# Block products for the output projection, and scores joined with the neighbouring group's attends, in a four-layer graph network on one core

## The chip, the cores and the metric

The kernel runs on one core of a Trainium2 chip. The core has five engines that run side by side and wait for one another through semaphores: TensorE (PE) for matrix products into PSUM (eight banks of 128 x 512 fp32), VectorE (DVE), ScalarE (ACT), GpSimd (POOL), and SyncE (SP), which here issues nearly all DMAs. The metric is device time of the one core in microseconds (us), the median of several executions. The profile is of one further execution.

## The reference

The input `x` holds 128 batches of 128 nodes with 512 features; `adj` is a 128 x 128 weighted adjacency matrix. Four layers follow one another, each with a residual sum and a layer norm, all in fp32:

```
# layer 0: graph convolution
x = layernorm(x + (adj @ x) @ W0 + bias0)
# layer 1: graph attention
h = x @ W1;  e = leaky_relu(h@a1 + (h@a2)^T) * adj
x = layernorm(x + elu(softmax(e) @ h + beta * h))
# layer 2: max over features; adj stands for both weights
A = adj @ x;  C = adj @ x + b
x = layernorm(x + max_j relu(A_j + (C - A)))
# layer 3: attention with 8 heads of 64, masked where adj == 0
q, k, v = split(x @ w_qkv)
o = softmax(mask(q k^T / 8)) @ v
o = o @ w_proj + b_proj
x = layernorm(x + o + layernorm(o) * gamma + beta)
```

## The kernel before

**Work.** A batch is one tile of 128 x 512. The work of a batch up to the end of layer 2 is `batch` (L906): load, `mixed_rows` or `mixed` (`adj @ x`, L276 to L309), a product with W0 (`product`, L269: four matmuls of 512 columns accumulated in one bank), layer norm (`layernorm_sums`, L243), two row sums with the attention vectors (L942), then layer 1 with a product of W1, layer 2 with one matmul (L974), and a transpose of the result (L989) that goes out to DRAM for layer 3. The tile itself is then written out to DRAM (`spill`, L892), apart from that of the last 8 batches (`KEPT`), which frees its buffer; `fetch` (L899) brings it back at the end.

**Layer 3** works on groups of four batches (31 of them, and two of two at the end). `gather` collects the four transposed tiles as a 2 x 2 block matrix, and forms four differences of blocks on GpSimd (L680). `section` (L685) computes q, k and v, each as seven products of blocks instead of eight (the Strassen-Winograd scheme: seven products of half-size blocks, sums of weights prepared once by `weight_sums`, copies on ScalarE at L743, sums on VectorE at L757, and a last copy at L813). `tiled` (L824) and `score` compute the scores of the four batches: two heads at a time in the two 64-row halves of the TensorE array. Each batch then adds the mask (L1006), takes the softmax (L1013 to L1034), and turns the result through DRAM (L1037 to L1046, `to_rows` and `from_rows`). `attend` (L862) multiplies with v, two batches in one block, in two 64-column halves of the array. `usual` (L1074) copies the output, multiplies by `w_proj` (`product`, four matmuls of 512 columns for each batch), adds the bias on VectorE (L1079), and ends with the two layer norms and the store; `last` (L1101) is the same for the last batch, cut in halves.

**Order.** The order of every engine is fixed when the kernel is built, by a planner (`Plan`, L63). Each chain of steps is a generator. `yield use(engine, work, buffer)` asks for an engine for so many estimated microseconds, and for a free buffer of a kind in `BUFS`. The planner always grants the request that can start first; among those that can start together the urgent one, then the lowest rank (usually the batch number). For TensorE it counts a request as ready up to 1 us (`MARGIN`) later than estimated. On the chip each engine runs its list in that order and waits for what isn't ready.

**Buffers.** Ten tiles `x` hold batches between load and spill; `t` (5) are scratch tiles; `qk` (4) and `v` (4) hold two groups; `z`, `e`, `et`, `eT` serve the attention of layer 1, `pt` the turned softmax. `layernorm_sums` writes its squares, which nobody reads, into a `t` tile (L248), and L942 does so too.

## Time and profile before

| | us |
|---|---|
| median of 3 runs (3197.40 to 3198.48) | 3198.22 |
| the profiled execution, its own time | 3195.69 |
| span of that execution | 3193.9 |
| mean granted TensorE clock, share of full speed | 0.992 |
| DMA: share of the 16 engines' time in the queue of SP | 46.7% |
| TensorE: three products of 512 columns a batch (L273), busy | 1376 |
| TensorE: blocks of q, k and v (L706), busy | 1257 |
| GpSimd: additions and subtractions of tiles (L266, L680), busy | 702 |
| VectorE: L942, 256 instructions, mean of one | 0.881 |

A line of the profile's groups names the source line, the engine, the operation, the tile that it writes and those that it reads (without their numbers), the shape, and the count of instructions; then the busy time of all, the mean of one in nanoseconds, and the idle time of the engine just ahead of them with what ended it. An fp32 matmul is recorded as two instructions, and as two weight loads ("PEld"). "128\*128" is the whole array, "64\*128" a half by rows, "128\*64" a half by columns. Matmuls are pipelined: the busy time of one overlaps that of the next, so the distance from start to start in the timeline is the better measure of cost.

### The profile page before, as it was taken

To read this page: it belongs to the slowest core of one execution; us is meant where nothing else is said; L and a number is where in the kernel's file an instruction comes from. 1 tells how busy PE (TensorE), PEld (TensorE's weight loads), DVE (VectorE), ACT (ScalarE), POOL (GpSimd) and SP (SyncE) were. 2 spreads that over 40 slices of the span, in tenths; PEclk is the share of its full clock that TensorE was granted. 3 is DMA by queue.
4 is the path that set the end of the run, shared out by engine and by line. 5 is a ranking of instruction groups with operands and counts; after the bars stand their busy time and mean duration, and the time that the engine had idled before them with its cause. 6 is when DMAs were issued, how large, how long until landed. Compare 5 with 4: busy or idle time off the path is not lost. (4 is left out here: it accounts for less than half of the span.)

```text
span 3193.9 us, 46192 instructions
## 1 busy us (share of the span) xinstructions
PE 3118.6 (98%) x14295; PEld 2063.0 (65%) x14295; DVE 2504.9 (78%) x5281; ACT 1768.6 (55%) x5143; POOL 1114.2 (35%) x1178
## 2 busy tenths in 40 slices
PE   8999999999999999999999999999999999999997
PEld 4566666666666676666666666666666666657785
DVE  7777878878878877787778787778678887877776
ACT  4565556555556655465645565546465556555553
POOL 5523343223343233333233423252323442342222
PEclk9999999999999999999999999999999999999998
DMA  4535455434563453555354644454534564344342
GB/s 164 146 111 153 116 152 150 134 122 136 141 167 116 135 153 100 165 145 144 121 132 123 170 123 141 121 146 128 160 103 133 139 175 123 117 126 115 101 138 94
DMA packets 766757, 429.47 MB, mean 134 GB/s; under 512 B 570032, under 2 KB 652336, under 8 KB 766512
## 3 DMA queue, kind: packets, MB, share of 16 engines
q1 hardware_dynamic: 766368, 426.26, 46.7%
q8 instruction: 115, 1.88, 0.3%
q14 instruction: 130, 1.06, 0.1%
q10 hardware_dynamic: 144, 0.26, 0.0%
HBM read 221.84 MB, written 204.54 MB: 133 GB/s over the span
## 5 line engine op out<-in xcount | busy, mean ns | idle before, releaser
L216 POOL TENSOR_TENSOR rstd<-ve,neghalf 128x1 f32<-128x1 f32 x640 | 402.2, 633 | 1473.2 <-ACT ve L255 1176.5
L273 PE MATMUL ps<-w_sb,yT 128*128 128x512 f32 x1952 | 874.9, 595 | 9.3 <-ACT yT L292 7.2
L273 PEld LDWEIGHTS ps<-w_sb,yT 128*128 128x128 f32 x1952 | 369.3, 191 | 410.6 <-issue 386.6
L706 PE MATMUL ps<-xT,wqkv_sb 128*128 128x256 f32 (+1 forms) x2112 | 474.0, 373 | 0.8 <-POOL xT L680 0.8
L273 PE MATMUL ps<-wproj_sb,v 128*128 128x512 f32 x1016 | 458.7, 603 | 14.6 <-ACT v L1061 9.9
L706 PEld LDWEIGHTS ps<-xT,wqkv_sb 128*128 128x128 f32 x2112 | 390.1, 190 | 79.0 <-issue 26.5
L1027 ACT ACTIVATE qk<-qk,nmx 128x128 f32<-128x128 f32 x1008 | 391.5, 391 | 25.8 <-DVE nmx L1013 25.5
L743 ACT COPY t<-ps 128x512 f32<-128x512 f32 (+1 forms) x297 | 168.5, 568 | 414.0 <-PE ps L706 230.7
L706 PE MATMUL ps<-xT,wsum_sb 128*128 128x256 f32 (+1 forms) x1584 | 357.4, 376 | 11.0 <-ACT t L743 10.9
L273 PEld LDWEIGHTS ps<-wproj_sb,v 128*128 128x128 f32 x1016 | 195.2, 193 | 251.1 <-issue 228.3
L706 PEld LDWEIGHTS ps<-xT,wsum_sb 128*128 128x128 f32 x1584 | 295.2, 192 | 76.5 <-issue 22.4
L942 DVE SCALAR_TENSOR_TENSOR t<-x,wa_rows 128x512 f32<-128x512 f32 x256 | 225.4, 881 | 56.6 <-ACT x L260 33.8
L250 ACT ACTIVATE t<-x,nm 128x512 f32<-128x512 f32 x263 | 187.8, 714 | 137.9 <-DVE nm L247 129.6
L680 POOL TENSOR_TENSOR xT<-xT 128x512 f32<-128x512 f32 (+1 forms) x132 | 173.1, 1315 | 220.2 <-PE ps L706 138.4
L706 PE MATMUL ps<-wqkv_sb,xT 128*128 128x256 f32 x1024 | 242.9, 380 | 0.0
L757 DVE TENSOR_TENSOR qk<-ps,t 128x256 f32<-128x256 f32 (+2 forms) x297 | 175.3, 620 | 84.5 <-PE ps L706 37.9
L706 PEld LDWEIGHTS ps<-wqkv_sb,xT 128*128 128x128 f32 x1024 | 192.2, 190 | 54.5 <-issue 25.2
L266 POOL TENSOR_TENSOR x<-x,beta_sb 128x512 f32<-128x512 f32 x128 | 178.8, 1399 | 115.9 <-DVE t L989 93.2
L260 ACT ACTIVATE x<-x,nmr,rstd 128x512 f32<-128x512 f32 x263 | 214.0, 814 | 8.8
L266 POOL TENSOR_TENSOR x<-x,bias_sb 128x512 f32<-128x512 f32 x128 | 176.1, 1386 | 118.0 <-PE ps L300 107.1
L266 POOL TENSOR_TENSOR xr<-xr,v 128x512 f32<-128x512 f32 x120 | 163.6, 1364 | 111.0 <-DVE v L1079 32.5
L1037 DVE STREAM_TRANSPOSE pt<-qk 128x1024 f32<-128x1024 f32 x128 | 158.4, 1238 | 42.0 <-DMA p_d<-pt 41.5
(109 smaller groups left out, 4833.0 us busy)
## 6 DMA issues: line engine op xcount, KB each, us to landing
p_d<-pt SPq DMA_DIRECT2D x128, 512.0 KB
qk<-p_d SPq DMA_DIRECT2D x128, 512.0 KB
x_d<-t SPq DMA_DIRECT2D x244, 256.0 KB
xT<-x_d SPq DMA_DIRECT2D x512, 64.0 KB
x<-in_x SPq DMA_DIRECT2D x127, 256.0 KB
x_s<-x SPq DMA_DIRECT2D x120, 256.0 KB
xr<-x_s SPq DMA_DIRECT2D x120, 256.0 KB
out<-xr SPq DMA_DIRECT2D x120, 256.0 KB
```

The costliest lines, as they stand in the source:

```text
L216: nc.gpsimd.tensor_tensor(rstd, ve, neghalf, op=ALU.pow)
L250: nc.scalar.activation(buf(b_sq, D), xb, AF.Square, bias=nm, accum_out=squares)
L260: nc.scalar.activation(xb, xb, AF.Identity, bias=nmr, scale=rstd)
L266: nc.gpsimd.tensor_tensor(dst, dst, other, op=ALU.add)
L273: nc.tensor.matmul(p, lhs(k), rhs(k), start=(k == 0), stop=(k == K - 1))
L680: nc.gpsimd.tensor_tensor(gr.xT[:, out, :, :n], gr.xT[:, a, :, :n], gr.xT[:, b, :, :n], op=ALU.subtract)
L706: nc.tensor.matmul(to, lhs, rhs, start=first and j == 0 and k == 0, stop=final and k == 1, skip_group_check=True,)
L743: nc.scalar.copy(held[1], p)
L757: nc.vector.tensor_tensor(c, a, b, op=ALU.add)
L942: nc.vector.scalar_tensor_tensor(buf(b_s, D), xb, 1.0, wa_rows[:, j, :], op0=ALU.mult, op1=ALU.mult, accum_out=gr.s[:, b, j : j + 1],)
L1027: nc.scalar.activation(pr[:, j, :], pr[:, j, :], AF.Exp, bias=nmx[:, j : j + 1], accum_out=sums[:, j : j + 1],)
L1037: nc.vector.transpose(pt.rearrange("p c h s -> p h c s"), pr.rearrange("p h (c r) -> p h c r", c=Q))
```

## The change

**The projection in pairs.** Two neighbouring batches of a group form the 2 x 2 block matrix that `section` forms of four. The scheme of seven products is taken out of `section` as `seven`, the block differences out of `gather` as `differences`, and `pair_product` uses both for a pair: seven products of 128 x 256 by 256 x 256. The last four batches (`PLAIN`) keep the four wide matmuls. The bias is now added on GpSimd. One block of `w_proj` is replaced by a difference when its sums are made, and loaded again ahead of the last two pairs (`wproj_again`).

**One tiled block.** `tiled` for group g now also runs the attends of group g-1 behind the scores of g, having waited for the softmax rows of all of g-1. In the last five groups (`APART`) the attends stay apart, each batch on its own.

**Buffers and ranks.** `x` goes from 10 to 7, `yT` from 4 to 3, `t` from 5 to 7; `z`, `e`, `et`, `eT` share 8 tiles `u`; the turned softmax takes two `t` tiles and goes out in two DMAs. At the start six batches are loaded into three idle `v` buffers (`GUESTS`). Squares overwrite the bank or tile read just before; L942's output goes into one fixed tile. The softmax takes a rank later by 10 (`SOFT`); only the last 4 batches stay unspilled. The small results of a norm share one tile. Estimates of some steps are changed, and TensorE's margin is 0.7 us from 2900 us on.

The core of the diff:

```diff
+APART = 5
-KEPT = 8
+KEPT = 4
+SEVEN1 = 0
+SEVENP = 1
+PLAIN = 4
+GUESTS = 6
+CLOSE = 2900
+SOFT = 10
+PROJ = 0
...
-    "x": 10, "xr": 2, "yT": 4, "z": 1, "e": 1, "et": 1, "eT": 3, "t": 5, "xT": 2, "v": 4,
-    "qk": 4, "pt": 1,
+    "x": 7, "xr": 2, "yT": 3, "u": 8, "t": 7, "xT": 2, "v": 4,
+    "qk": 4, "y": 0, "c": 2,
...
-        early = min(MARGIN, r["ready"] / 20) if engine == "PE" and order else 0.0
+        spare = MARGIN if r["ready"] < CLOSE else 0.7
+        early = min(spare, r["ready"] / 20) if engine == "PE" and order else 0.0
...
-        b_sq = yield use("ACT", 1.2, "t")
-        squares = small.tile([P, 1], F32, name="squares")
-        nc.scalar.activation(
-            buf(b_sq, D), xb, AF.Square, bias=nm, accum_out=squares
-        )
-        give(b_sq)
...
+        yield use("ACT", 1.2)
+        nc.scalar.activation(buf_or_bank(unread), xb, AF.Square, bias=nm, accum_out=squares)
+        give(unread)
...
-        for i in range(8, BUFS["x"]):
+        for i in range(8, BUFS["x"] + GUESTS):
             yield from load(i)
...
-            plan.start(tiled(gr, None, range(size)), rank)
-            for b in range(0, size, ATTENDS):
-                bs = tuple(range(b, min(b + ATTENDS, size)))
-                for bs in (bs,) if g < len(sizes) - 1 else tuple((b,) for b in bs):
-                    plan.start(attend(gr, bs), first)
+            plan.start(tiled(gr, groups.get(g - 1) if g - 1 < len(sizes) - APART else None, range(size)), rank)
+            if g >= len(sizes) - APART:
+                for b in range(size):
+                    plan.start(attend(gr, (b,)), first)
...
+    def seven(rank, bx, wide, time, multiply, into, finished, have, pieces, slow=0.0):
...
+        x = bank(bx, D)[:, :wide]
+        multiply(x, A11, B11, True)
+        m1 = keep(x)
+
+        bz = yield use("PE", time, "ps", late=0.2)
+        z = bank(bz, D)[:, :wide]
+        multiply(z, A12, B21, True, True)
+        plan.start(release(add(z, m1, 0, 0), bz), rank)
+
+        yield m1[0]
+        yield have[T2]
+        yield use("PE", time, late=0.2)
+        multiply(x, S2, T2)
+        u2 = keep(x)
...
+    def differences(blocks, have, used, time, rank):
+
         for out, a, b, when, t in (
             (T3, B22, B12, None, T3), (T1, B12, B11, None, T1),
...
+            yield use("POOL", time, urgent=True)
+            nc.gpsimd.tensor_tensor(blocks(out), blocks(a), blocks(b), op=ALU.subtract)
+            done(have[t], 0.1)
+
+    def pair_product(rank, s, ready, blocks, release, out, finished):
...
+        def multiply(p, w, block, first=False, final=False):
+            w, t = weight(s, w), blocks(block)
+            for k in range(2):
+                nc.tensor.matmul(
+                    p, t[:, k], w[:, k, :], start=first and k == 0, stop=final and k == 1,
+                    skip_group_check=True,
+                )
...
+        plan.start(differences(blocks, have, used, 0.75, rank), rank)
+        token = yield use("PE", 0.0, "c", late=0.0)
+        bx, *slots = yield use("PE", 0.87, lambda: ("ps", "t", "t"), late=0.2)
+        out.extend(buf(slot, D) for slot in slots)
+        out.append(slots)
+        yield from seven(
+            rank, bx, D // 2, 0.87, multiply, into, finished, have, lambda *tiles: [tiles],
+        )
+        give(token)
...
+        yield i + SOFT
         yield use("DVE", 1.22)
...
-        yield use("SP", 0.5, late=4.0)
-        to_rows(pt.rearrange("p c h s -> p c (h s)"), scratch)
-        give(bt)
+        for j, pt in enumerate(turned):
+            yield use("SP", 0.5, late=4.0 * j)
+            to_rows(
+                pt.rearrange("p c h s -> p c (h s)"),
+                scratch[:, :, j * H // 2 * S : (j + 1) * H // 2 * S],
+            )
+        for bt in halves:
+            give(bt)
...
+        if SEVENP and gr.first + 2 * h < NB - PLAIN:
+            if h not in gr.extra:
+                gr.extra[h] = None
+                plan.start(projection(gr, h, i + PROJ), i + PROJ)
+            done(gr.copied[h])
+            yield gr.projected[h][b % 2]
+            o, slot = gr.p[h][b % 2], gr.p[h][2][b % 2]
+            biased = Event()
+            plan.start(pool_add(o, bproj_sb, biased), i)
+            yield biased
+            yield from normed(i, o, lambda: give(slot), fetched)
+        else:
+            yield from (last if i == NB - 1 else usual)(
+                i, oT, v, lambda: gr.read(("v", b // 2), 2), fetched
+            )
```

## The prediction

> **What bounds the kernel now.** I read busy times first, then the groups by shape, the granted clock and waits, then TensorE's timeline.

> ```profile
> PE 3118.6 (98%) x14295; PEld 2063.0 (65%) x14295; DVE 2504.9 (78%) x5281; ACT 1768.6 (55%) x5143; POOL 1114.2 (35%) x1178
> PE   8999999999999999999999999999999999999997
> ```

> TensorE is busy in every slice, so a microsecond of its work is a microsecond of time, unless a new wait replaces it. Its idle time is 75.3 us (3193.9 - 3118.6). The waits that release it sum to 14 us before 110 us, 41 us up to 3100 and some 11 us behind, and none stands out: the longest total is 10.9 us ("ACT t L743").

> Part of the start, from the table by stretches (length, then busy time and count of PE, PEld, DVE, ACT and POOL, then clock, DMA share, GB/s): 5.5 us idle, and a clock of 0.89.

> ```profile
> 60.00:100.00 40.00, 34.52 (x112) 18.66 (x112) 34.88 (x89) 23.34 (x58) 16.17 (x16) 0.89 0.19 60
> ```

> Busy time of pipelined matmuls overstates, so I price TensorE from one start to the next in its timeline (start, length, line, count of instructions; one fp32 matmul shows as two):

> ```profile
> 1546.89 3.60 PE L273 MATMUL ps<-w_sb,yT 128*128 128x512 f32 x8
> 1550.42 3.84 PE L856 MATMUL ps<-qk 64*128 64x128 f32 x64
> 1554.19 1.12 PE L974 MATMUL ps<-x,adjT 128*128 128x512 f32 x2
> 1555.15 3.60 PE L273 MATMUL ps<-w_sb,yT 128*128 128x512 f32 x8
> 1558.59 1.95 PE L281 MATMUL ps<-eT,x 128*128 128x128 f32 x16
> 1560.37 1.89 PE L706 MATMUL ps<-wqkv_sb,xT 128*128 128x256 f32 x8
> 1562.10 7.03 PE L273 MATMUL ps<-w_sb,yT 128*128 128x512 f32 x16
> ...
> 1581.01 3.62 PE L706 MATMUL ps<-xT,wqkv_sb 128*128 128x256 f32 x16
> 1584.56 1.97 PE L877 MATMUL ps<-qk,v 128*64 128x128 f32 x32
> 1586.46 1.99 PE L706 MATMUL ps<-xT,wqkv_sb 128*128 128x256 f32 x8
> 1588.29 3.60 PE L273 MATMUL ps<-wproj_sb,v 128*128 128x512 f32 x8
> ```

> A 512-column product is 3.44 us (1555.15 to 1558.59). Ahead of a tiled block it is 3.53 (1546.89 to 1550.42).

> **Part 1, the projection.** Two batches now cost two L273 products, 6.88 us. The seven products are two matmuls of 256 columns each, four recorded instructions: the form that the value section has in groups of two.

> ```profile
> 3088.99 1.03 PE L706 MATMUL ps<-wqkv_sb,xT 128*128 128x256 f32 x4
> 3089.86 1.95 PE L706 MATMUL ps<-xT,wqkv_sb 128*128 128x128 f32 x16
> ```

> That is 0.87 us each, 6.09 for seven, so a pair saves 0.79. All but the last four batches go this way: 62 x 0.79 = **48.7 us** off TensorE.

> [...] A pair goes from 16 weight loads to 28, all on full rows, and the row of L706 prices one at 190 ns[...]. The row decides: eight instructions of 256 columns last 1.73 us (1560.37 to 1562.10), eight of 512 columns 3.44, with as many loads. Per column the one costs what the other does, so the doubled loads are hidden; I take 48.7.

> The other engines, from the groups by shape:

> ```profile
> L1079 DVE TENSOR_TENSOR v<-ps,bproj_sb 128x512 f32<-128x512 f32 x127 | 86.8, 684 | 51.2 <-PE ps L273 48.7 <-ACT x L260 1.7
> L757 DVE TENSOR_TENSOR v<-ps,t 128x256 f32<-128x256 f32 x6 | 2.5, 410 | 1.1 <-ACT t L743 0.7 <-PE ps L706 0.4
> L743 ACT COPY t<-ps 128x256 f32<-128x256 f32 x18 | 6.6, 369 | 14.5 <-PE ps L706 7.6 <-DVE nm L247 5.9 <-DVE qk L757 0.8
> L680 POOL TENSOR_TENSOR xT<-xT 128x256 f32<-128x256 f32 x8 | 6.2, 771 | 17.9 <-DMA xT<-x_d 10.0 <-PE ps L706 7.8
> ```

> VectorE loses 124 bias adds (-84.8 us) and gets three sums a pair, 186 x 0.41 = +76.3. ScalarE gets four copies a pair, 248 x 0.37 = +91, to 1860 (59%). GpSimd gets the bias adds (124 x 1.386 = 172), four differences a pair (248 x 0.771 = 191) and four weight sums (6): 1114 to 1483, 47%. None reaches TensorE's time. The seven products wait on one another's copies; sections of other groups and layers 0 to 2 lie between, as they do for L706 now.

> GpSimd's additions slow VectorE. Sorting the timeline by whether a large GpSimd add overlaps it, L942 takes 1.23 us beside one (87 of 256) and 0.70 without, L1091 1.42 against 0.75, L1087 1.08 against 0.74. Large GpSimd work grows by half (about 700 to 1060 us), so half as many again are hit: 43 x 0.53 + 25 x 0.67 + 28 x 0.34, about 50 us with L1034. [...] VectorE's sum is about 2567 (82% of the forecast) by the row[...]. Either stays under TensorE, so I charge nothing; without that cover the 50 us would be paid.

> **Part 2, scores and attends in one block.** Sixteen full-size 128-column matmuls take 1.78 us (1558.59 to 1560.37), so 0.89 us per batch of scores or attends. A score block of four takes 3.77, 0.21 over; the product ahead pays 0.09 and the matmul behind 0.10 (1554.19 to 1555.15 is 0.96; 0.86 elsewhere). Together 0.41. An attend block of two takes 1.90, 0.12 over, and its neighbours pay 0.10 each: 0.32. One place has them adjoining:

> ```profile
> 3068.63 1.16 PE L856 MATMUL ps<-qk 64*128 64x128 f32 x16
> 3069.72 3.71 PE L877 MATMUL ps<-qk,v 128*64 128x128 f32 x64
> 3073.37 14.00 PE L273 MATMUL ps<-wproj_sb,v 128*128 128x512 f32 x32
> ```

> Scores 1.09 (0.20 over), attends 3.65 (0.09 over), 0.10 on either side: 0.49. A group now pays 0.41 + 2 x 0.32 = 1.05, so merging saves 0.56. There are 28 merges, 15.7 us. In the last five groups attends go singly, seven more blocks, 2.2 back. Net **13.5 us**. Now 11 score blocks are broken after three batches for want of banks. Unbroken blocks would return 4 us more; were each merged block broken into single attends, 28 x 1.2 = 34 would be lost. VectorE empties two banks in 1.37 us (681 ns each, L1006) while TensorE uses two per 0.89 us of scores, then one per 0.89 of attends, so the banks nearly keep up: I leave the share broken as it is.

> The block has a new wait: group g's attends stand behind the softmax rows of all four batches and group g+1's q and k. They come a group period (100 us) later, holding q/k and v buffers longer. Behind the wait on TensorE is everything in its order; the planner fills it with layers 0 to 2 of seven batches.

> **Part 3, buffers.** Pairing each line's k-th execution (batches 24 to 111), a batch needs 109 us from load to L934 and 132 from L934 to its spill (L895). Most of the 109 is waiting after landing: the work itself, load 3.9, L300 0.86, L303 0.70, two DMA hops of 4.1 and 3.9, product 3.44, sum 0.7, is some 18. So a buffer is needed for about 150 us. Ten give 250, seven 171 at the new pace: 21 us of slack, enough, cost 0.

> Until 100 us TensorE idles 14 us, mostly in waits for the first attention matrices (L281) with no other batch loaded. Six guests in the v buffers make 13 loads instead of 10: three more first-layer products, 3 x (0.89 + 3.44) = 13 us of filling. Ends 0 and 13; they load behind much else, so I take **6**.

> **Small edits.** The softmax's output goes out in two DMAs: 128 more issues on SP at 0.38 us, with SP often waiting itself (L336), and two transposes of about 0.70 for one of 1.24, +20 us of covered VectorE. Only the last group shows it: +1 us (0 to 3). Squares written over read banks hold a bank some 1.5 us longer and relieve t; no row shows ScalarE writing there. The nearest, its reads (581 ns against 714 into SBUF), put it between -0.13 and +0.13 us each: 0 where ScalarE has 40% spare. Softmax at a later rank and four more spilled batches: 0.

> **Sum.** 48.7 + 13.5 + 6 - 1 = 67 us off the profiled execution's 3195.7 (span 3193.9, 1.8 around it): 3128.5. The median shown is 2.5 above that execution, so **3131**.

> **Rivals.** *B, half goes into waits.* Whole-group waits, banks held longer and the products' mutual waits double the 41 us of mid-run idle: 3131 + 41 = 3172. For it: fewer batches in flight.[...]
> *C, slower: x starves.* A buffer is held longer than seven batch periods of the old pace, 7 x 24.97 = 174.8 us. From there holding time / 7 is the pace; at 178 us it gives 25.4 x 128 = 3255. For it: 132 us of the chain were seen with ten buffers and a busier GpSimd lengthens them. Against: the wait of L942 to L961 (66 us on average, 38 at least) has slack.
> *D, more.* The start fills wholly (7 more) and the mid-run idle halves (20): 3104. For it: gaps now come from single late copies and DMAs. Against: nothing in the change shortens these chains.

> **Chances.** Forecast 0.55, B 0.22, C 0.08, D 0.15. A measurement here tells 0.2% (6.4 us) from nothing; B's far end touches it. So faster 0.90, same 0.02, slower 0.08. The range reaches from a little under D to a little over B: 3100 to 3176. It takes in the broken blocks (+34) and leaves out C.

> **What would show it.** Right: TensorE still at 97% or more; seven times four instructions per pair at 0.87; some 28 scores-to-attends changes without full-size work between; 50 us more VectorE. Wrong: loads waiting on spills with TensorE idle on L300 (C), TensorE waiting for copies of the projection or for the softmax's DMA inside the merged block (B), 256-column products above 0.95[...], or merged blocks in pieces.

## The result, and the profile after

The changed kernel takes 3157.86 us (median of four, 3154.84 to 3159.49) beside 3198.14 for the kernel before on the same chip: a ratio of 0.9873, interval 0.9856 to 0.9890. It is 40 us faster. The forecast was 67 us faster, 3131, with a range of 3100 to 3176; the time lies inside, and the gain is 60% of the one forecast. The profiled execution shows the same difference: its span is 3153.0 us instead of 3193.9, 40.9 less.

The page of the changed kernel, busy times and TensorE by slices:

```profile
span 3153.0 us, 48736 instructions
PE 3058.7 (97%) x15039; PEld 2205.0 (70%) x15039; DVE 2550.1 (81%) x5470; ACT 1851.3 (59%) x5391; POOL 1512.5 (48%) x1554
PE   9899999999999999999999999999999999999996
```

TensorE's busy time fell by 59.9 us. Its idle time (span less busy) rose by 19.0, from 75.3 to 94.3. At an equal granted clock (0.992) these two make up the 40.9.

The idle time by place, from the table by stretches of the changed kernel (length, busy time and count of PE, PEld, DVE, ACT and POOL, then clock, DMA share, GB/s):

```profile
0.00:200.00 200.00, 181.85 (x627) 104.67 (x628) 154.30 (x371) 100.71 (x237) 104.73 (x103) 0.97 0.49 145
200.00:3053.00 2853.00, 2802.01 (x13901) 2042.08 (x13900) 2316.51 (x4947) 1697.50 (x4982) 1364.24 (x1407) 1.00 0.50 137
3053.00:3153.00 100.00, 74.80 (x514) 58.27 (x513) 79.30 (x154) 53.13 (x173) 43.52 (x46) 0.90 0.42 129
```

That is 18.2 us idle in the first 200, 51.0 between, 25.2 in the last 100. The kernel before, cut the same way, has 15.2, 39.1 and 21.0:

```profile
200.00:3093.90 2893.90, 2854.82 (x13079) 1890.90 (x13078) 2284.43 (x4791) 1625.44 (x4762) 997.06 (x1056) 1.00 0.48 135
3093.90:3193.90 100.00, 78.99 (x501) 57.31 (x500) 70.73 (x138) 40.86 (x120) 29.25 (x35) 0.89 0.36 116
```

So 3 us of the added idle time is in the first 200, 12 in the middle and 4 at the end.

TensorE's waits in the changed kernel (line that waited, releaser; total, times, longest in us):

```profile
PE ps L304 <- DMA x<-in_x: 14.6, 9, 2.8
PE ps L869 <- ACT t L732: 11.0, 7, 3.2
PE ps L277 <- DMA yT<-x_d: 7.3, 5, 2.9
PE ps L277 <- DMA wproj_sb<-in_L_gnn_w_proj: 6.0, 1, 6.0
PE ps L277 <- ACT yT L296: 5.1, 2, 3.3
PE ps L1102 <- ACT x L264: 4.8, 6, 1.8
PE ps L825 <- ACT u L732: 4.4, 4, 3.1
```

The first is new. With ten buffers no first-layer matmul (L304, which was L300) waited for its load; with seven, nine did. Pairing executions as before, a batch now needs 45 us from its load to its first sum (L1027, which was L934; 109 before): most of the lead is used up, and some loads come just too late. The third was 0.5 us before. The fourth is new too, the reload of the weight block near the end. The products of the projection (L825) wait 4.4 us in the whole run.

### The profile page after: what moved, and what is told of

The parts are those of the page before. It is cut to its first block, busy times and chain, and to the rows that moved or that the text cites. A ratio compares the mean times of both kernels' runs of the same rounds, so it can differ in the third digit from the quotient of the medians.

```text
span 3153.0 us, 48736 instructions
## 1 busy us (share of the span) xinstructions
PE 3058.7 (97%) x15039; PEld 2205.0 (70%) x15039; DVE 2550.1 (81%) x5470; ACT 1851.3 (59%) x5391; POOL 1512.5 (48%) x1554
## 3 DMA queue, kind: packets, MB, share of 16 engines
q8 instruction: 120, 1.97, 0.3%
## 5 line engine op out<-in xcount | busy, mean ns | idle before, releaser
L228 POOL TENSOR_TENSOR sums<-sums,neghalf 128x1 f32<-128x1 f32 x383 | 256.9, 671 | 590.7 <-ACT sums L260 566.9
L869 PE MATMUL ps<-xT,wqkv_sb 128*128 128x256 f32 (+1 forms) x2112 | 478.8, 375 | 2.6 <-DVE t L307 2.2
L869 PEld LDWEIGHTS ps<-xT,wqkv_sb 128*128 128x128 f32 x2112 | 393.5, 191 | 88.6 <-issue 32.9
L869 PE MATMUL ps<-xT,wsum_sb 128*128 128x256 f32 (+1 forms) x1584 | 356.9, 376 | 12.9 <-ACT t L732 8.5
L869 PEld LDWEIGHTS ps<-xT,wsum_sb 128*128 128x128 f32 x1584 | 294.9, 192 | 77.3 <-issue 20.5
L732 ACT COPY t<-ps 128x512 f32<-128x512 f32 x279 | 160.7, 578 | 257.9 <-PE ps L869 168.2
L228 POOL TENSOR_TENSOR n<-n,neghalf 128x1 f32<-128x1 f32 x257 | 173.2, 674 | 215.6 <-DVE n L223 194.5
L258 ACT ACTIVATE ps<-x,sums 128x512 f32<-128x512 f32 x244 | 167.0, 684 | 133.7 <-DVE sums L256 133.0
L869 PE MATMUL ps<-wqkv_sb,xT 128*128 128x256 f32 x1024 | 241.5, 380 | 0.0
L1034 DVE SCALAR_TENSOR_TENSOR unread_dve<-x,wa_rows 128x512 f32<-128x512 f32 x244 | 212.1, 869 | 24.6 <-ACT x L264 19.6
L746 DVE TENSOR_TENSOR qk<-ps,t 128x256 f32<-128x256 f32 (+1 forms) x279 | 168.5, 635 | 76.7 <-PE ps L869 41.6
L869 PEld LDWEIGHTS ps<-wqkv_sb,xT 128*128 128x128 f32 x1024 | 193.5, 190 | 44.5 <-issue 17.7
L270 POOL TENSOR_TENSOR t<-t,bproj_sb 128x512 f32<-128x512 f32 x124 | 174.9, 1415 | 102.3 <-ACT t L792 68.2
L264 ACT ACTIVATE x<-x,sums 128x512 f32<-128x512 f32 x247 | 201.0, 814 | 8.3
L270 POOL TENSOR_TENSOR xr<-xr,t 128x512 f32<-128x512 f32 x124 | 175.5, 1417 | 40.3 <-DMA xr<-x_s 31.2
L1156 ACT ACTIVATION_READ_ACCUMULATOR qk<-qk,nmx 128x1 f32 x1008 | 191.0, 189 | 0.0
```

The costliest lines, as they stand in the source:

```text
L228: nc.gpsimd.tensor_tensor(rstd, ve, neghalf, op=ALU.pow)
L258: nc.scalar.activation(buf_or_bank(unread), xb, AF.Square, bias=nm, accum_out=squares)
L264: nc.scalar.activation(xb, xb, AF.Identity, bias=nmr, scale=rstd)
L270: nc.gpsimd.tensor_tensor(dst, dst, other, op=ALU.add)
L732: nc.scalar.copy(held[1], p)
L746: nc.vector.tensor_tensor(c, a, b, op=ALU.add)
```

## The experiments

The draws of chip differ (the kernel before has medians of 3192 to 3198 beside these runs), so kernels are compared by their ratio to the kernel before. All twelve are in one table, each with its profiled execution. "Idle" is TensorE's in the first 200 us, between, and in the last 100. "Half clock" is worked out from the trace's record of TensorE's clock, which holds two values, 1.0 and 0.5 of full speed: it is half of the busy time that falls into stretches at 0.5, as an estimate of the time lost in them (a product of L825 in the changed kernel takes 1.86 us to the next start at 0.5, 3111.73 to 3113.59, and 0.87 at 1.0). "Work" is the busy time without that loss.

| kernel | ratio (interval) | span, us | PE busy | half clock | work | idle |
|---|---|---|---|---|---|---|
| before | 1 | 3193.9 | 3118.6 | 19.0 | 3099.6 | 15 + 39 + 21 |
| changed | 0.9873 (0.9856 to 0.9890) | 3153.0 | 3058.7 | 18.1 | 3040.6 | 18 + 51 + 25 |
| e1, wide projection | 1.0059 (1.0042 to 1.0076) | 3212.5 | 3112.1 | 27.5 | 3084.6 | 15 + 62 + 24 |
| e2, attends apart | 1.0151 (1.0131 to 1.0170) | 3237.7 | 3104.7 | 33.9 | 3070.8 | 19 + 85 + 30 |
| e3, third part alone | 1.0149 (1.0120 to 1.0178) | 3237.3 | 3133.5 | 29.2 | 3104.3 | 14 + 65 + 25 |
| e4, softmax not late | 1.0031 (1.0023 to 1.0039) | 3196.4 | 3072.0 | 31.3 | 3040.7 | 16 + 82 + 26 |
| e5, before, 7 x | 1.0064 (1.0049 to 1.0079) | 3212.6 | 3117.8 | 20.1 | 3097.7 | 33 + 33 + 28 |
| e6, before, 9 x | 1.0173 (1.0157 to 1.0188) | 3245.8 | 3126.4 | 28.1 | 3098.3 | 25 + 68 + 27 |
| e7, before, softmax late | 1.0226 (1.0211 to 1.0242) | 3268.4 | 3142.4 | 42.8 | 3099.6 | 14 + 90 + 21 |
| e8, before, joined block | 1.0071 (1.0054 to 1.0088) | 3215.6 | 3113.3 | 28.7 | 3084.6 | 15 + 53 + 34 |
| e9, before, margin 0.99 | 1.0012 (1.0005 to 1.0018) | 3195.1 | 3119.1 | 22.4 | 3096.7 | 15 + 40 + 20 |
| e10, changed, margin 0.99 | 0.9890 (0.9875 to 0.9905) | 3160.0 | 3060.9 | 21.5 | 3039.4 | 18 + 52 + 29 |
| e11, changed, margin 1.01 | 0.9954 (0.9939 to 0.9969) | 3176.0 | 3057.8 | 17.4 | 3040.4 | 26 + 60 + 33 |
| e12, changed, reload early | 0.9868 (0.9853 to 0.9883) | 3155.4 | 3067.5 | 27.5 | 3040.0 | 19 + 48 + 21 |

Kernels with the same matmuls have the same work within 3 us: 3096.7 to 3099.6 for the kernel before and e5, e6, e7 and e9, and 3039.4 to 3040.7 for the changed one and e4, e10, e11 and e12 (which differs by one pair).

### Each part undone (e1 to e4)

**e1.** The projection alone goes back:

```diff
-SEVENP = 1
+SEVENP = 0
```

> The changed kernel with its projection back in four wide matmuls for each batch, the bias on VectorE and no reload of a weight block. Theory T (the part prices on TensorE hold, and the 27 us short of the forecast were lost at the start, in loads of x and at the end): TensorE's busy time rises by 48 to 3107, and the median by 48 less the 6 us of the reload's wait, to about 3200. Theory R (the seven products give part of their gain back through waits on one another's copies and through GpSimd's added work): without them idle time falls too, by 15 or more, and the median is 3185 or less.

Busy time rose by 53.4 us, idle time by 6. The ratio went up by 0.0186, 59 us of 3198. R, which had the seven products give some of their gain back in waits, falls: idle time rose without them, although the wait for the reload is gone. Of the 53 us of busy time 9 are half clock. TensorE's work rose by 44.0, which is 5 less than the 48.7 of the forecast; the rest of the 59 us is waiting and what the clock loses by it, and can be the draw of the order (below).

**e2.** All attends apart, one block for each batch:

```diff
-APART = 5
+APART = 40
```

> The changed kernel with every batch's attends in a block of their own, in all groups. By the prices of the tile shapes on TensorE a merged group costs 0.49 us and one in five blocks 0.41 + 4 x 0.32 = 1.69, so 28 x 1.2 = 34 us more: T expects 3192, with TensorE's busy time up by about 30. R (the merged block pays for its price with idle time, since it waits for four softmax rows): idle time falls by 10 or more and the median stays under 3182. If moving the attends also shifts what waits for what, the idle time rises instead and the median goes over 3205.

The ratio rose by 0.0278, 89 us. T had 34, R is wrong in sign, and the last sentence of the expectation is what came: idle time rose, by 39 us. Busy time rose by 46, of which 30 are work, as T priced it, and 16 are half clock. One wait of e2 is more than the added idle time:

```profile
PE ps L970 <- DMA qk<-p_d: 54.3, 28, 4.8
```

In the changed kernel the attends waited for that DMA twice, 2.4 us in all, and both times in the last groups, where they stand apart. No joined block waited for it: behind the scores of the next group, the attends find the softmax landed.

**e3.** Both large parts undone; what is left is the third part.

```diff
-SEVENP = 1
+SEVENP = 0
...
-            plan.start(tiled(gr, groups.get(g - 1) if g - 1 < len(sizes) - APART else None, range(size)), rank)
-            if g >= len(sizes) - APART:
-                for b in range(size):
-                    plan.start(attend(gr, (b,)), first)
+            plan.start(tiled(gr, None, range(size)), rank)
+            for b in range(0, size, ATTENDS):
+                bs = tuple(range(b, min(b + ATTENDS, size)))
+                for bs in (bs,) if g < len(sizes) - 1 else tuple((b,) for b in bs):
+                    plan.start(attend(gr, bs), first)
```

> Both large parts undone (wide projection, attends in pairs apart from the scores); what is left of the change are its buffers, ranks and the start. T: the third part is worth little, -5 to +5 against the kernel before, so 3193 to 3203. R (seven buffers of x, late softmax and full-time banks cost time that the two large parts then hide): slower than before, 3215 or more, with more than 100 us of idle time on TensorE.

R holds: 1.5% slower than the kernel before, about 48 us, with 104 us of idle time. Of the three causes that R names, the trace points to the late softmax; it doesn't measure the other two. The longest wait is again that of the attends:

```profile
PE ps L971 <- DMA qk<-p_d: 30.9, 20, 4.1
```

**e4.** The softmax at its batch's own rank:

```diff
-SOFT = 10
+SOFT = 0
```

> The changed kernel with the softmax at the batch's own rank instead of one later by ten. The forecast priced the later rank at 0: T expects 3158 within 8. The rival: with seven buffers of x the softmax's 6 us a batch on VectorE stand ahead of the layers that free the buffers, and TensorE runs dry of first layers; then 3190 to 3260, with TensorE's idle time well over 120 us and its waits on loads of x or on layer norms.

The ratio rose by 0.0158, 50 us; the rival holds. Its idle time of 124 us is only just over the 120 named, but TensorE's waits on loads of x more than doubled, from 14.6 to 36.2 us:

```profile
PE ps L304 <- DMA x<-in_x: 36.2, 7, 12.8
```

### Each part alone, in the kernel before (e5 to e8)

**e5**, seven buffers of x:

```diff
-    "x": 10, "xr": 2, ...
+    "x": 7, "xr": 2, ...
-KEPT = 8
+KEPT = 4
...
-        for i in range(4, 8):
+        for i in range(4, 7):
```

> The kernel before with 7 buffers of x in place of 10 and the last 4 batches unspilled (at the start it loads seven batches ahead of the weights). The forecast read 21 us of slack per buffer out of the trace and priced this at 0: then 3193 to 3203 beside the 3198 of before, and no waits of L300 on loads. Theory X (the seven buffers are what the third part costs, since a batch keeps its buffer for the planner's order and not for its bare chain): 3225 to 3255, with 20 us or more of added idle time on TensorE.

**e6**, nine buffers (`"x": 9`):

> The kernel before with 9 buffers of x, nothing else. If the slack is a threshold (theory of the forecast), the same as before within 5 us. If each buffer costs by itself (X), a part of the loss of seven, +8 to +20 us.

e5 lost 20 us by its ratio, but not where X had it. In the middle it idles 33 us, less than the kernel before with ten buffers. Most of the loss is at the start (33 us idle instead of 15; the end has 7 more), where TensorE has seven batches and nothing else:

```profile
62.12 3.64 PE L281 MATMUL ps<-eT,x 128*128 128x128 f32 x16 [24.38 <-DMA eT<-e_d]
```

Nine buffers then cost more than seven, 1.7%. So the loss doesn't grow with the buffers taken away, and X falls. The forecast's threshold of slack doesn't explain e6 either, and it had no wait of L300 on loads in e5, where there are two, of 4.5 us in all.

**e7**, the late softmax:

```diff
+        yield i + 10
         yield use("DVE", 1.22)
         nmx = small.tile([P, H], F32, name="nmx3")
```

> The kernel before with the softmax's VectorE and ScalarE work at a rank later by 10, nothing else. Theory S (the late softmax is what the third part costs, as the attends apart then wait for its DMA): 3215 or more, with TensorE's wait of the attends (L877) on the softmax's DMA over 25 us instead of 9. X: within 8 us of before.

2.3% slower, 72 us, and the wait that S named:

```profile
PE ps L877 <- DMA qk<-p_d: 47.4, 22, 5.7
```

**e8**, the joined block:

```diff
-            plan.start(tiled(gr, None, range(size)), rank)
...
+            plan.start(tiled(gr, groups.get(g - 1) if g - 1 < len(sizes) - 5 else None, range(size)), rank)
+            if g >= len(sizes) - 5:
+                for b in range(size):
+                    plan.start(attend(gr, (b,)), first)
```

> The kernel before with the joined block of scores and attends alone (the last five groups apart, as in the change). By the prices of the blocks alone TensorE saves 13 us: 3185. In the other kernels the joined block gained 29 us, because it took the attends out of waits on the softmax's DMA; the kernel before has only 9 us of those: then 3175 to 3190. The rival: the block's wait for four softmax rows costs more in a kernel whose softmax isn't ranked for it: over 3205.

0.7% slower, 23 us. TensorE's work fell by 15.0, close to the 13.5 of the forecast, but idle time rose by 27 and the half clock by 10. The median of 3218 us lies in the rival's range; the wait that the rival named is not what the trace shows:

```profile
PE ps L876 <- DMA qk<-p_d: 26.4, 3, 20.0
PE ps L876 <- DVE qk L1005: 18.1, 3, 6.6
PE ps L281 <- DVE qk L1005: 12.1, 3, 4.5
```

The wait of 20.0 for the softmax's DMA is one of the last group, whose attends stand apart. In the middle TensorE waits 30 us for VectorE's sums with the mask (L1005), which empty the banks of the scores.

### The draw of the order (e9 to e11)

Each of the eight edits left a kernel slower than the one before. That raises a question: is each loss that of its edit, or does any edit draw a new order, and the two kernels had good ones? Three kernels change the planner's margin by 1% and nothing else. That alone reorders thousands of places in the lists.

```diff
-MARGIN = 1.0
+MARGIN = 0.99
```

(e9 in the kernel before, e10 in the changed one; e11 has 1.01.)

> The kernel before with the planner's margin at 0.99 us in place of 1.00. No work is added or removed, but the planner's list order changes in thousands of places. Theory O (the order drawn by the planner is worth tens of us, and the kernel before was a lucky draw, so that undoing or doing one thing measures mostly a new draw): 10 to 60 us slower than before, with idle time of TensorE up by 10 or more. Theory X (the losses of the four kernels made from the one before belong to what was changed in each): within 5 us of before.

> The changed kernel with the margin at 0.99 us. O: the same work (TensorE's busy time within 8 us of 3059) but 5 to 40 us more idle time, so 3163 to 3200; the gain that is left is the change's own, apart from the draw. X: within 5 us of 3158.

> The changed kernel with the margin at 1.01 us, a second draw of its order. O: again 3163 to 3200, and not the same as with 0.99. X: within 5 us of 3158.

e9 moved by 0.12% (4 us) and e10 by 0.17% (5 us): by these O falls. e11 moved by 0.81%, 26 us, without a change of busy time (3057.8), so O holds there. Of its idle time, one piece stands out. The table by stretches of e11, near the end:

```profile
3100.00:3132.00 32.00, 31.54 (x216) 24.93 (x215) 23.12 (x54) 14.42 (x42) 20.83 (x20) 1.00 0.42 132
3132.00:3155.00 23.00, 0.90 (x6) 0.50 (x6) 17.04 (x28) 8.30 (x18) 2.16 (x4) 0.63 0.38 121
```

For 22 us TensorE has nothing left but the attends of the last group, while VectorE works off norms and that group's softmax. In the changed kernel projections of earlier pairs still lie over it. e10 has such a wait too, 18.3 us, and makes most of it good elsewhere. So a draw is worth between 4 and 26 us in three tries, which don't bound it. The losses of e1, e2 and e4 against the changed kernel, and of e3, e6 and e7 against the one before, are more than any draw seen here; those of e5 and e8 are not. For e2, e3, e4 and e7 the trace also shows one wait, repeated, behind the loss. The loss of e6 has no such explanation, and may be a larger draw.

### The reload (e12)

```diff
-PLAIN = 4
+PLAIN = 6
```

> The changed kernel with the last six batches on the wide matmuls instead of four. The order differs from the changed kernel's only in the last rows of each engine (15 of TensorE's 2900), so no new draw enters. The reload of the weight block then comes one pair earlier. Theory: the 6.0 us for which TensorE waited for it go, and one pair pays 0.8 us more: 3153, 5 us under the changed kernel. Rival: the end is set by the last group's softmax and its DMA anyway, and the wait moves there: within 1.5 us of it.

By time the two can't be told apart: 0.9868 and 0.9873, each with a half interval of 0.0015 or more. The trace can tell, since nothing but the last rows of each engine's list differs. First the changed kernel's end, then that of e12; both from the same block of attends (start, length, line, count of instructions, wait ahead of it):

```profile
3094.70 1.09 PE L970 MATMUL ps<-qk,v 128*64 128x128 f32 x16
...
3113.59 1.79 PE L825 MATMUL ps<-wproj_sb,v 128*128 128x256 f32 x4
3121.40 5.64 PE L277 MATMUL ps<-wproj_sb,v 128*128 128x512 f32 x8 [6.02 <-DMA wproj_sb<-in_L_gnn_w_proj]
3126.97 1.09 PE L970 MATMUL ps<-qk,v 128*64 128x128 f32 x16
```

```profile
3101.03 1.09 PE L970 MATMUL ps<-qk,v 128*64 128x128 f32 x16
...
3112.03 1.98 PE L970 MATMUL ps<-qk,v 128*64 128x128 f32 x16 [3.52 <-DMA qk<-p_d]
3113.93 15.82 PE L277 MATMUL ps<-wproj_sb,v 128*128 128x512 f32 x32
3130.89 1.09 PE L970 MATMUL ps<-qk,v 128*64 128x128 f32 x16 [1.14 <-DMA qk<-p_d]
```

The wait of 6.02 is gone. From that block to the end of the span the changed kernel takes 58.3 us and e12 54.4: 3.9 less, of the 5 expected. Part of the wait moved to the softmax's DMA, as the rival had it. Up to that block e12's profiled execution is 6 us longer under the same order. It is the slowest of e12's four, and over its whole span it lost 27.5 us at half clock instead of 18.1.

No version was found that is measurably faster than the changed kernel. e10's order, without the 18 us wait at its end, might be one; it was not tried.

## Why the forecast was right, and where its sum was off

The direction held, and rival C (slower, with x starving) did not come. The sum was 67 us, and the profiled executions differ by 40.9: 26 too good. The work of the two large parts was priced well; three quarters of the 26 are in the step that was put at nothing, the buffers and ranks. That the time lies in the range is in part luck. The third part alone cost 48 us where the sum had a gain of 5, and the two large parts then won 88 instead of 62, so two misses cancel in part; and the changed kernel in the order of e11 would be at 3183 us (0.9954 of 3198), outside the range. By its own steps:

**Projection, -48.7: right.** (62 x 0.79 is 49.0; the sum has 0.3 less.) The products run as priced. This is the changed kernel's timeline at a joined block:

```profile
1508.02 1.16 PE L949 MATMUL ps<-qk 64*128 64x128 f32 x16
1509.12 3.71 PE L970 MATMUL ps<-qk,v 128*64 128x128 f32 x64
1512.76 1.99 PE L869 MATMUL ps<-wsum_sb,xT 128*128 128x256 f32 x8
1514.59 3.60 PE L277 MATMUL ps<-w_sb,yT 128*128 128x512 f32 x8
1518.02 1.03 PE L825 MATMUL ps<-wproj_sb,v 128*128 128x256 f32 x4
1518.89 1.95 PE L285 MATMUL ps<-u,x 128*128 128x128 f32 x16
```

The product of L825 takes 0.87 us to the next start, as in the sum; the median of 215 such lone products is 0.86. That is a quarter of the 3.43 us of eight instructions of 512 columns (1514.59 to 1518.02), which have half as many weight loads per column. So the 12 further loads of a pair show in no start: paid in full they would be 12 x 0.19 = 2.28 us a pair, an estimate from the 190 ns of a weight load of L706 in the kernel before. By e1 the part is worth 44.0 us of work; what the 5 us short of the sum are is not shown.

**Joined block, -13.5: its price right, its worth not.** Behind the scores the attends of four batches take 3.64 (1509.12 to 1512.76), 0.08 over, where the sum had 0.09. Of the 31 score blocks of full groups 15 are broken, instead of 11. Together with the projection TensorE's busy time was to fall by 62.2; it fell by 59.9, and the work by 59.0. What the forecast missed is that the block also hides the softmax's DMA. With attends apart and the softmax late, TensorE waits for it 20 to 28 times, 31 to 54 us (e2, e3, e7); with both in place, 2.4 us. The late softmax in turn was priced at 0 and is worth 50 us in the changed kernel (e4), and costs 72 in the one before (e7). So the late softmax needs the joined block, and has no price of its own. What it wins in the changed kernel is mostly loads of x that come in time (e4). Beside the kernel before the block could win little of the softmax's wait, since that kernel had only 9 us of it.

**Other engines, 0: right.** VectorE was put at 2567 and is 2550, ScalarE 1860 and 1851, GpSimd 1483 and 1512. The groups by shape have the rows that the sum used:

```profile
L270 POOL TENSOR_TENSOR t<-t,bproj_sb 128x512 f32<-128x512 f32 x124 | 174.9, 1415 | 102.3 <-ACT t L792 68.2 <-DVE n L215 10.8 <-DVE t L746 10.7
L812 POOL TENSOR_TENSOR v<-v 128x256 f32<-128x256 f32 x186 | 141.4, 761 | 196.5 <-PE ps L825 189.5
L746 DVE TENSOR_TENSOR t<-ps,u 128x256 f32<-128x256 f32 x186 | 76.8, 416 | 67.9 <-PE ps L825 32.0 <-ACT u L732 17.2 <-ACT qk L792 4.7
L258 ACT ACTIVATE ps<-x,sums 128x512 f32<-128x512 f32 x244 | 167.0, 684 | 133.7 <-DVE sums L256 133.0
```

GpSimd's adds hit 91 of the 256 instructions of L1034 (87 before, 130 expected), which take 1.20 us beside one and 0.70 without. The 50 us taken from the rows came near: VectorE rose by 45 us in all, and in it 8 us more for two transposes in place of one (the forecast had 20) and 8 less for the sums of the projection cancel. The rise is not on L1034, which takes 224.9 us beside 225.4 before. ScalarE's squares into a bank take 684 ns instead of 714, within the bounds set.

**The start, -6: right in the stretch it priced.** The step was about the first 100 us, and there idle time fell by 4.9, from 14.3 to 9.4. The two stretches before, then after:

```profile
0.00:100.00 100.00, 85.73 (x303) 49.34 (x304) 74.78 (x185) 48.89 (x119) 50.01 (x50) 0.95 0.41 145
100.00:200.00 100.00, 99.02 (x418) 65.43 (x417) 75.00 (x170) 53.40 (x147) 37.90 (x38) 1.00 0.50 129
0.00:100.00 100.00, 90.63 (x323) 50.76 (x324) 77.39 (x189) 52.09 (x128) 58.68 (x55) 0.98 0.43 150
100.00:200.00 100.00, 91.22 (x305) 53.91 (x304) 76.91 (x182) 48.62 (x109) 46.05 (x49) 0.97 0.55 141
```

The six guests fill the start that seven buffers alone leave empty (e5). The reading of the waits was off, though: 5.2 of the 14 us were for the attention matrices (L281), and 7.6 were products behind ScalarE's copies (L273). Behind 100 us idle time rose by 7.8, in waits of up to 2 us for layer norms (L1102), differences of blocks (L869) and attention matrices (L285). No run shows what causes these.

**Buffers and ranks, 0: the term that was mis-sized.** Between the first and the last 100 us TensorE idles 20 us more (7.8 up to 200 and 11.9 behind), where the sum had none: three quarters of the miss. The 21 us of slack per buffer were an average: enough in the kernel before, whose middle did not suffer from seven (e5), but in the changed one nine loads come late, 14.6 us, and in e10, e11 and e12 as well (14.1, 18.9 and 11.8). The number of buffers alone does not explain it: e5 has the same 45 us from load to first sum, with 4.5 us of late loads. What else makes them late stays open. The third part alone makes the kernel about 48 us slower (e3); the other two then win 88, and the difference is the 40 measured. How much of the 48 is the late softmax without its block, how much banks, buffers and a draw, is not settled: e6 cost 1.7% for one buffer, and no theory here explains that. Two edits of this part were not tried alone: `yT` with three tiles instead of four, and the DRAM tiles of the turned batches (`x_d`) with four instead of 16. TensorE's waits for that path (`yT<-x_d`) rose from 0.5 to 7.3 us.

**The end, +1: 4 instead.** The reload stood in the diff, but the sum had no term for it; it made TensorE wait 6.02 us, 3.9 of which e12 takes back. So the 26 us are 20 from the middle, 3 from the end, 1 from the start, and 2 of TensorE's busy time: 59.9 instead of 62.2.

Rival B was nearest to what happened, with 20 us of new waits in mid-run in place of its 41. But of the causes it named, the whole-group waits did not come, the waits for VectorE's mask sums, which free banks, are 7 us (1 before), and the products' waits on one another's copies (L825) are 4.4; the largest new wait, 14.6 us, is the one of rival C, loads of x.

## What to carry to other kernels

Where an engine is at 98%, price what is taken off it from start to start in the timeline: the sum made so came within 4% of the fall in busy time. Then look for what else each step sets in order: a block that is joined also moves who waits for whom, and a rank that frees one queue starves another, so an edit can be worth much beside another and cost when alone. And before a small loss is put down to an edit of a planned order, change something that adds no work: here that moved the time by 4, 5 and 26 us.

## What the runs showed of the hardware

Some waits of TensorE cost more than their length here. The wide product behind the 6.02 us wait took 5.57 us to the next start (3121.40 to 3126.97), where one ahead of a tiled block takes 3.53 (1546.89 to 1550.42 in the kernel before): 2 us more. The mean clock granted in that stretch is 0.64, and 0.36 of 5.57 us is 2.0:

```profile
3121.40:3126.97 5.57, 5.57 (x8) 2.20 (x9) 0.76 (x2) 0.00 (x0) 2.40 (x3) 0.64 0.61 168
```

Across whole runs it shows as busy time. e7 has the same matmuls as the kernel before, in as many blocks, and its busy time is 23.8 us higher. The loss at half clock is 42.8 us instead of 19.0, which is the whole difference. e5 is the counterpart: with its 24.38 us wait at the start the mean clock of the first 200 us is 0.93 instead of 0.97, and that of the whole span 0.987 instead of 0.992, but its busy time doesn't rise (3117.8 instead of 3118.6), and its loss at half clock is 20.1.
